# Normalised scores ahead of the queries' maximum, and gate sums in two float32r passes, in a fused attention and feed-forward kernel

## The chip, the cores and the metric

The kernel runs on one core of a Trainium2 chip. The metric is the device time of one execution in microseconds. A core has engines with queues of their own: PE (matrix products; its weight loads are listed apart as PEld), DVE, ACT and POOL (elementwise work), and SP, which here starts the DMAs. Each engine works through its queue in order and waits on semaphores for what other engines make.

## The reference

A block of a transformer on 2 sequences of 1024 tokens with 512 features, in float32:

```
x = x + layernorm(attention(layernorm(x)))
x = x + layernorm(ffn(layernorm(x)))

attention: q = x Wq (32 heads of 128), k = x Wk, v = x Wv (8 heads, each shared by 4 query heads)
  linear part:  qs = softmax(q), ks = softmax(k), gates gs = log_sigmoid(k) / 16
                per token: S = S * exp(gs) + ks v^T;  o_lin = qs S
  window part:  rope on q and k, softmax over the tokens of the own and the previous
                block of 64, masked to a distance of 64, times v
  o = 0.5 * window + 0.5 * o_lin, rounded to bfloat16, then times Wo
ffn: weights quantised to 16 levels in blocks of 64 and back;
     silu(x w1^T) * (x w2^T), then times w3^T
```

## The kernel before

**Work.** The attention part takes 8 key heads times 2 sequences times 8 stretches of 128 tokens, 128 *chunks* in all, in one loop over `n`. A chunk is one key head with its four query heads (`GRP`) on 128 tokens. Keys are made for two chunks at a time (`CB` = 2), so even and odd chunks differ: an even chunk makes the key products and key softmax of the pair to come (`key_products`, `key_softmax`), an odd chunk finishes them (`key_gates`, `key_decays`, `key_transposes`). Below, the numbering is from 0: `n` = 0 is even.

**Order.** Nothing plans the order. The attention's instructions are issued through `InOrder`, which keeps each engine's queue in program order, so the order of the calls in the loop is the order in each queue. All of these instructions are recorded on line 116, so the profile is read by tile names:

- `query_products(n + 1)`: PE makes `pq` (4 products of 512 columns); ACT copies it to `q`; POOL does the rope, `qtmp<-q,fcos`, two halves `qr<-q,fsin`, and `qr<-qr,qtmp`; DVE takes the negated maximum `nmq<-pq`.
- `query_exps`: four ACT exps of `pq` with `nmq` as bias. `query_softmax`: DVE `rsq`, then `qs<-pq,rsq`.
- `scores(n)`: PE `ps<-kT,qrT`. `score_masks`: DVE adds `fwin`, then the maximum `nms`. `score_exps`: four ACT exps of `ps`. `score_softmax`: DVE reciprocal `rss`, then the normalised scores `sw<-ps,rss`.
- `linear(n)`: PE `pa<-qh,kT`, `pa<-qh,khz`, `ot<-qh,S`. `mix`: PE transposes `sw` into `pa` (`pa<-ident,sw`); DVE masks `pa` to `A`. `values`: PE `ot<-A,vm`, `ot<-A,kv`. `heads`, `rounded_heads`: ACT `ob`, `oc`. `project`: PE `py<-wop,oc`, eight float32r products; `collect`: DVE `yacc`.
- `key_softmax`: ACT `kv`, then POOL rope `kr`, then POOL copies `vm`; DVE `nmk`; ACT `gate` = ln(1 + exp(-k)) and the exps `ke`. `key_gates`: PE `pg<-gate,fmid`, a float32 product of 256 columns with the constant `mid` (values of 0 and plus or minus 1/16), which sums the gates over tokens; ACT `ex` and `pg` exps. `key_decays`: DVE `kh`. `key_transposes`: PE `pt<-ident,kr`, `pt<-ident,kh`, `pg<-ident,ex`; ACT `kT`, `eq`, `em`.
- `query_transposes`: PE `tr<-ident,qr`, ACT copies it to `qrT`; PE `tq<-ident,qs`, which DVE turns into `qh` in the next chunk.
- `state_products`, `next_state`: PE `pS`, DVE `S`; the last chunk of a sequence has none.
- `signs` and `steps` spread the rounding of the feed-forward weights over the chunks: ACT signs `zs`, DVE steps on `zp` and `zm`. `part_weights` splits the output weights on POOL into float32r high and low parts (`wop`), in four chunks of each key head.

A float32 product stands in the trace as two instructions, a float32r one as one. PSUM pools have two buffers each (`pmm`: `pk`, `pq`, `pg`; `ptr`: `pt`, `tr`, `tq`; `psc`: `ps`, `pa`, `pS`; `po`: `ot`, `py`). After the attention comes the feed-forward part, with products of 512 columns.

Of the kernel before, what the change touches and what calls it, by code (L numbers as in the profile page):

```python
# [11 lines left out]
F32 = mybir.dt.float32  # L12
# [107 lines left out]
def sandwich_kernel(ctx: ExitStack, tc: tile.TileContext, x, wq, wk, wv, wo, w1, w2, w3, out, con):  # L120
# [141 lines left out]
    def fast_attention():  # L262

        with ExitStack() as attn:
# [62 lines left out]
            def load_const(name, shape, dtype, src):  # L327
                t = fc.tile(shape, dtype, name=name)
                nc.sync.dma_start(t, src)
                return t  # L330

            cosT = load_const("fcos", [P, NCH, D], F32, con["fcos"].rearrange("(c p) d -> p c d", p=P))
            sinT = load_const("fsin", [P, NCH, D], F32, con["fsin"].rearrange("(c p) d -> p c d", p=P))
            mid = load_const("fmid", [P, P], F32, con["fmid"])
            fwin = load_const("fwin", [P, 2, 4, P], BF16, con["fwin"])
            causal = load_const("fcausal", [P, 4 * P], F32, con["fcausal"])
            qb = load_const("fbounds", [P, 16], F32, con["bounds"])
# [17 lines left out]
            def row_max(src, n, tag):  # L355

                nm = fs.tile([P, n], F32, tag=f"nm{tag}", name=f"nm{tag}")
                vector.tensor_reduce(nm, src, AX.X, ALU.max, negate=True)
                return nm
# [29 lines left out]
            def key_softmax(n):  # L389

                c0, K = chunks[n][2], keys[n // CB]
                pk, before = K["pk"], K["before"]
                kv = kbuf.tile([P, CB, 2 * D], F32, tag="kv", name="kv")
                scalar.copy(kv, pk)
                k, v = kv[:, :, 0:D], kv[:, :, D : 2 * D]
                kr = ktmp.tile([P, CB, D], F32, tag="kr", name="kr")
                tmp = ktmp.tile([P, CB, D], F32, tag="tmp", name="tmp")
                rope(kr.unsqueeze(2), tmp.unsqueeze(2), k.unsqueeze(2), c0, CB, 1)

                vm = kbuf.tile([P, CB, D], F32, tag="vm", name="vm")  # L400
                gpsimd.tensor_copy(vm[0:W], v[0:W])
                gpsimd.tensor_copy(vm[W:P, 1:CB, :], v[W:P, 0 : CB - 1, :])
                if before is None:
                    gpsimd.memset(vm[W:P, 0, :], 0.0)
                else:
                    gpsimd.tensor_copy(vm[W:P, 0, :], before["v"][W:P, CB - 1, :])
                nm = row_max(pk[:, :, 0:D], CB, "k")

                gate = ktmp.tile([P, CB, D], F32, tag="gate", name="gate")
                scalar.activation(gate, pk[:, :, 0:D], AF.Exp, scale=-1.0)  # L410
                scalar.activation(gate, gate, AF.Ln, bias=1.0)
                ke = ktmp.tile([P, CB, D], F32, tag="ke", name="ke")
                sm = row_exps(ke, pk[:, :, 0:D], nm, CB, "k")
                K.update(v=v, vm=vm, kr=kr, gate=gate, ke=ke, sm=sm)

            def key_gates(n):

                K = keys[n // CB]
                pg = pmm.tile([P, 2, CB, P], F32, tag="mm", name="pg")
                product(pg[:, 0].rearrange("p j d -> p (j d)"), lhsT=mid, rhs=K["gate"].rearrange("p j d -> p (j d)"), start=True, stop=True)  # L420
                ex = ktmp.tile([P, CB, D], F32, tag="ex", name="ex")
                scalar.activation(ex, pg[:, 0], AF.Exp)
                ek = pg[:, 0]
                scalar.activation(ek, ek, AF.Exp, scale=-1.0)
                K.update(ex=ex, ek=ek, pe=pg[:, 1])
# [41 lines left out]
            def query_products(n):  # L467

                g, b, c = chunks[n]
                ci = b * NCH + c  # L470
                pq = pmm.tile([P, GRP, D], F32, tag="mm", name="pq")
                for kt in range(KT):
                    product(pq.rearrange("p h d -> p (h d)"), lhsT=xnT[:, kt, ci * P : (ci + 1) * P], rhs=weights[g][0][:, kt, :], start=kt == 0, stop=kt == KT - 1)
                q = q1p.tile([P, GRP, D], F32, tag="q", name="q")
                scalar.copy(q, pq)
                qr = q1p.tile([P, GRP, D], F32, tag="qr", name="qr")
                tmp = q1p.tile([P, GRP, D], F32, tag="qtmp", name="qtmp")
                rope(qr.unsqueeze(1), tmp.unsqueeze(1), q.unsqueeze(1), c, 1, GRP)
                Q[n] = {"pq": pq, "qr": qr, "nm": row_max(pq, GRP, "q")}

            def query_exps(n):

# [5 lines left out]
                vector.tensor_tensor(qs, Q[n]["pq"], rs.unsqueeze(2).to_broadcast([P, GRP, D]), ALU.mult)  # L488
                Q[n]["qs"] = qs

            def query_transposes(n):

                tr = ptr.tile([P, GRP, P], F32, tag="tr", name="tr")
                for h in range(GRP):
                    transpose(tr[:, h, :], Q[n]["qr"][:, h, :])
                qrT = q2p.tile([P, 2, GRP * W], F32, tag="qrT", name="qrT")
                scalar.copy(qrT.rearrange("p n (h t) -> p n h t", h=GRP), tr.rearrange("p h (n t) -> p n h t", n=2))
                tq = ptr.tile([P, GRP, P], F32, tag="tr", name="tq")
                for h in range(GRP):
                    transpose(tq[:, h, :], Q[n]["qs"][:, h, :])  # L500
                Q[n] = {"qrT": qrT, "tq": tq}

            def query_decays(n):
                j = n % CB
# [145 lines left out]
            key_softmax(0)  # L650
            key_sums(0)
            query_products(0)
            key_gates(0)
            key_decays(0)
            query_exps(0)
            query_softmax(0)
            key_transposes(0)
            query_transposes(0)

            BEGIN = (NCI - 2 * CB) // 2  # L660
            for n in range(N_):
                g, b, c = chunks[n]
                inputs = list(range(2 * CB + 2 * n, min(2 * CB + 2 * n + 2, NCI)))
                even = n % CB == 0
                more, keys2 = n + 1 < N_, n + CB < N_


                scores(n)
                if n:
                    rounded_heads(n - 1)  # L670
                score_masks(n)
                query_decays(n)
                if n:
                    next_state(n - 1)
                signs(2 if even else 1, n)
                steps(1, n)
                score_exps(n)
                if more:
                    query_products(n + 1)
                if even:  # L680
                    if more:
                        query_exps(n + 1)
                    signs(3, n)
                    score_softmax(n)
                    steps(1, n)
                    linear(n)
                    if keys2:
                        key_products(n + CB)
                    query_softmax(n + 1)
                    steps(1, n)  # L690
                    for ci in inputs[:1]:
                        input_norms(ci)
                    if keys2:
                        key_softmax(n + CB)
                    mix(n)
                    steps(1, n)
                    if keys2:
                        key_sums(n + CB)
                    if n:
                        project(n - 1)  # L700
                        collect(n - 1)
                    query_transposes(n + 1)
                    signs(1, n)
                    values(n)
                    heads(n)
                    steps(2, n)
                    for ci in inputs[1:]:
                        input_norms(ci)
                else:
                    if more:  # L710
                        key_gates(n + 1)
                        query_exps(n + 1)
                    signs(2, n)
                    score_softmax(n)
                    if more:
                        key_decays(n + 1)
                    linear(n)
                    mix(n)
                    if more:
                        query_softmax(n + 1)  # L720
                    project(n - 1)
                    collect(n - 1)
                    for ci in inputs[:1]:
                        input_norms(ci)
                    if more:
                        key_transposes(n + 1)
                    values(n)
                    if more:
                        query_transposes(n + 1)
                    heads(n)  # L730
                    steps(2, n)
                    for ci in inputs[1:]:
                        input_norms(ci)
                state_products(n)
                for ci in inputs:
                    input_transposes(ci)
                if b == 1 and c == 0 and g + 1 < KVH:
                    weights[g + 1] = load_weights(g + 1)
                if b == 1 and 2 <= c < 2 + GRP and g + 1 < KVH:
                    part_weights(g + 1, c - 2)  # L740
# [460 lines left out]
```

## Time and the profile before

| | |
|---|---|
| median of 3 runs | 2220.66 us (2218.14 to 2221.49) |
| the profiled execution | 2219.97 us |
| its span, first to last instruction | 2218.1 us |
| first scores (`ps`) of chunk 0, of chunk 127 | 55.5 us, 1701.1 us |
| even chunk, odd chunk, median from `ps` to `ps` | 13.84 us, 12.01 us |
| mean granted TensorE clock | 0.987 |

Some busy time on each engine stands in the page: PE 96%, DVE 67%, ACT 62%, POOL 42%. The lengths that the trace gives to matmuls overlap each other, so how long PE needs for a group is read from its start to the start of the next group. In a list of waits, `A <- B` means that engine and tile A sat idle until B ended, with the total, the number of times and the longest in us; in a timeline the idle time ahead of an instruction stands in brackets.

### The profile page before, as it was taken

The numbers are of one execution on the slowest core, as the hardware profiler recorded it, in microseconds if no ns is written. First come the engines' busy times: TensorE is split into PE (matmuls) and PEld (weight loads), VectorE is DVE, ScalarE is ACT, GpSimd is POOL, SyncE is SP. The second block draws the span as 40 slices with busy tenths as digits, with TensorE's granted clock in tenths as the row PEclk, the third lists the DMA queues.
The fourth block names the chain that finished last, engine by engine and source line by source line (L and its number), as shares of the span: only waits on it lengthen the run. The fifth ranks groups of instructions, "written<-read, shape, count | busy, mean of one in ns | idle before, by whom it ended". The sixth has DMA issues, their size and how long they took to land.

```text
span 2218.1 us, 27608 instructions
## 1 busy us (share of the span) xinstructions
PE 2132.0 (96%) x8948; PEld 1411.8 (64%) x8948; DVE 1484.3 (67%) x2822; ACT 1366.7 (62%) x3944; POOL 942.7 (42%) x1290
## 2 busy tenths in 40 slices
PE   4999999999999999999999999999998799999998
PEld 2667777777777767767777767776775454444443
DVE  3657788888778878778888878778886524232212
ACT  2568788787787888887778888788885210101000
POOL 3445555655465556446645655565553101000000
PEclk7999999999999999999999999999999899999999
DMA  5100100010010001000100010000000410000000
GB/s 200 34 15 10 58 11 15 25 48 10 9 41 26 15 15 58 10 10 10 58 14 15 21 49 11 12 10 17 10 12 19 143 44 34 5 29 1 19 0 21
DMA packets 45192, 64.52 MB, mean 29 GB/s; under 512 B 3632, under 2 KB 19632, under 8 KB 45040
## 3 DMA queue, kind: packets, MB, share of 16 engines
q1 hardware_dynamic: 45040, 62.67, 8.6%
q8 instruction: 73, 1.20, 0.2%
q14 instruction: 79, 0.65, 0.1%
HBM read 50.01 MB, written 12.65 MB: 28 GB/s over the span
## 4 chain that ended last, share of the span: by engine, by line
PE 67%; DVE 14%; ACT 14%; issue 2%; POOL 1%; DMA 1%; ACTq 0%; DVEq 0%; POOLq 0%; SPq 0%
PE py L116 9%; PE pq L116 8%; PE pk L116 7%; PE pgate L1125 7%; PE pf L1143 7%; PE pup L1125 7%; ACT ps L116 6%; PE ot L116 5%; PE ps L116 5%; PE pa L116 5%; DVE nmq L116 3%; DVE nms L116 2%; DVE ps L116 2%; DVE sw L116 2%; ACT q L116 2%; PE tr L116 2%
## 5 line engine op out<-in xcount | busy, mean ns | idle before, releaser
L116 PE MATMUL pq<-wq,xnT 128*128 128x512 f32 x1024 | 462.0, 594 | 0.0
L116 POOL TENSOR_TENSOR qtmp<-q,fcos 128x512 f32<-128x512 f32 x128 | 162.2, 1267 | 594.1 <-ACT q L116 594.1
L116 PEld LDWEIGHTS pq<-wq,xnT 128*128 128x128 f32 x1024 | 185.5, 191 | 184.5 <-issue 184.5
L116 ACT ACTIVATE zs<-xw,fbounds 128x512 bf16<-128x512 f32 (+3 forms) x416 | 288.2, 725 | 0.0
L116 PE MATMUL py<-wop,oc 128*128 128x512 f32 x1024 | 270.7, 406 | 1.3 <-ACT oc L116 1.3
L152 POOL TENSOR_TENSOR rstd<-ve,mhalf 128x1 f32<-128x1 f32 x64 | 35.8, 567 | 530.1 <-DVE ve L150 525.4
L116 ACT ACTIVATE ps<-ps,nms 128x128 f32<-128x128 f32 x512 | 175.0, 342 | 106.9 <-DVE nms L116 89.7
L116 PE MATMUL pk<-wkv,xnT 128*128 128x256 f32 x1024 | 233.8, 382 | 0.0
L1128 ACT ACTIVATE sg<-pgate 128x512 f32<-128x512 f32 (+1 forms) x44 | 26.3, 597 | 324.9 <-PE pgate L1125 324.9
L116 PEld LDWEIGHTS pk<-wkv,xnT 128*128 128x128 f32 x1024 | 196.2, 192 | 47.2 <-issue 14.1
L116 ACT ACTIVATE pq<-pq,nmq 128x128 f32<-128x128 f32 x512 | 175.1, 342 | 75.7 <-DVE nmq L116 63.2
L116 PEld LDWEIGHTS py<-wop,oc 128*128 128x128 f32 x1024 | 183.3, 189 | 36.5 <-ACT oc L116 1.7
L116 POOL TENSOR_TENSOR qr<-q,fsin 128x256 f32<-128x256 f32 x256 | 205.8, 825 | 0.0
L116 DVE SCALAR_TENSOR_TENSOR zp<-zp,zs 128x512 f32<-128x512 f32 (+3 forms) x224 | 195.4, 872 | 9.4 <-ACT zs L116 5.0
L116 POOL TENSOR_TENSOR qr<-qr,qtmp 128x512 f32<-128x512 f32 x128 | 166.4, 1300 | 9.8
L116 DVE TENSOR_TENSOR ps<-ps,fwin 128x512 f32<-128x512 f32 x128 | 89.3, 697 | 120.2 <-PE ps L116 119.5
L116 DVE SCALAR_TENSOR_TENSOR zm<-zm,zs 128x512 f32<-128x512 f32 (+3 forms) x192 | 163.3, 851 | 5.7 <-ACT zs L116 3.0
L116 DVE TENSOR_REDUCE nmq<-pq 128x4 f32<-128x512 f32 x128 | 88.5, 691 | 112.6 <-ACT q L116 112.6
L1125 PE MATMUL pgate<-x2T,w1T 128*128 128x512 f32 (+1 forms) x352 | 160.9, 595 | 0.0
L1125 PE MATMUL pup<-x2T,w2T 128*128 128x512 f32 (+1 forms) x352 | 158.2, 592 | 0.0
L1143 PE MATMUL pf<-w3T,hT 128*128 128x512 f32 (+1 forms) x352 | 151.8, 592 | 0.0
L116 PE MATMUL ps<-kT,qrT 128*128 128x128 f32 x1024 | 140.9, 281 | 9.9 <-ACT qrT L116 4.9
(125 smaller groups left out, 4077.2 us busy)
## 6 DMA issues: line engine op xcount, KB each, us to landing
wq<-in_L_attn_Wq_dram SPq DMA_DIRECT2D x8, 1024.0 KB, 6.3
wo<-in_L_attn_Wo_dram SPq DMA_DIRECT2D x8, 1024.0 KB, 5.1
xw<-in_L_ffn_w_dram SPq DMA_DIRECT2D x20, 256.0 KB, 2.6
dq<-zp SPq DMA_DIRECT2D x20, 256.0 KB, 2.0
row<-dq SPq DMA_DIRECT2D x20, 256.0 KB, 2.8
x<-_attn_hidden_states_dram SPq DMA_DIRECT2D x16, 256.0 KB, 2.8
xc<-_attn_hidden_states_dram SPq DMA_DIRECT2D x16, 256.0 KB, 2.7
out_dram<-res SPq DMA_DIRECT2D x16, 256.0 KB, 2.0
```

Of the source, the lines that this page charges most:

```text
L116: return lambda *args, **kwargs: self.tc.keep_in_program_order(getattr(self.engine, name)(*args, **kwargs))
L152: nc.gpsimd.tensor_tensor(rstd, ve, mhalf, ALU.pow)
L1125: nc.tensor.matmul(pg[:n, :], lhsT=wT[:, kt, f * P : f * P + n], rhs=x2T[:, kt, :], start=kt == 0, stop=kt == KT - 1)
L1128: nc.scalar.activation(sg[:n, :], ps[0][:n, :], AF.Sigmoid)
L1143: nc.tensor.matmul(pf, lhsT=hT[:n, f, m * P : (m + 1) * P], rhs=w3T[:n, f, :], start=f == 0, stop=f == NFT - 1)
```

## The change

Three things, in the attention part alone:

- In odd chunks `score_softmax(n)` (DVE `rss`, `sw`) comes ahead of the queries' maximum `nmq`, which has a function of its own, `query_max`; `key_decays` moves ahead of `signs(2, n)`. In even chunks the order stays.
- `query_transposes` is split in two. In odd chunks the rope part (`tr`, `qrT`) comes before `values`, and the softmax part (`tq`) stays behind it. `qrT` has one buffer instead of two.
- The gates are split on POOL into a float32r high part and the exact rest (`gates`, a copy and a subtraction, between `kr` and `vm`), and `pg` is the sum of two float32r products with `mid`, which is made float32r once by a DVE copy.

```diff
-            mid = load_const("fmid", [P, P], F32, con["fmid"])
+            mid = fc.tile([P, P], F32R, name="mid")
+            nc.vector.tensor_copy(mid, load_const("fmid", [P, P], F32, con["fmid"]))
...
                 rope(kr.unsqueeze(2), tmp.unsqueeze(2), k.unsqueeze(2), c0, CB, 1)
+                nm = row_max(pk[:, :, 0:D], CB, "k")
+
+
+                gate = ktmp.tile([P, CB, D], F32, tag="gate", name="gate")
+                scalar.activation(gate, pk[:, :, 0:D], AF.Exp, scale=-1.0)
+                scalar.activation(gate, gate, AF.Ln, bias=1.0)
+                gates = ktmp.tile([P, 2, CB, D], F32R, tag="gates", name="gates")
+                gpsimd.tensor_copy(gates[:, 0], gate)
+                gpsimd.tensor_tensor(gates[:, 1], gate, gates[:, 0].bitcast(F32), ALU.subtract)
...
-                nm = row_max(pk[:, :, 0:D], CB, "k")
-
-                gate = ktmp.tile([P, CB, D], F32, tag="gate", name="gate")
-                scalar.activation(gate, pk[:, :, 0:D], AF.Exp, scale=-1.0)
-                scalar.activation(gate, gate, AF.Ln, bias=1.0)
...
-                product(pg[:, 0].rearrange("p j d -> p (j d)"), lhsT=mid, rhs=K["gate"].rearrange("p j d -> p (j d)"), start=True, stop=True)
+                for i in range(2):
+                    product(pg[:, 0].rearrange("p j d -> p (j d)"), lhsT=mid, rhs=K["gates"][:, i].rearrange("p j d -> p (j d)"), start=i == 0, stop=i == 1)
...
-                Q[n] = {"pq": pq, "qr": qr, "nm": row_max(pq, GRP, "q")}
+                Q[n] = {"pq": pq, "qr": qr}
+
+            def query_max(n):
+                Q[n]["nm"] = row_max(Q[n]["pq"], GRP, "q")
...
-            def query_transposes(n):
+            def rope_transposes(n):
 
                 tr = ptr.tile([P, GRP, P], F32, tag="tr", name="tr")
                 for h in range(GRP):
                     transpose(tr[:, h, :], Q[n]["qr"][:, h, :])
-                qrT = q2p.tile([P, 2, GRP * W], F32, tag="qrT", name="qrT")
+                qrT = q2p.tile([P, 2, GRP * W], F32, tag="qrT", name="qrT", bufs=1)
                 scalar.copy(qrT.rearrange("p n (h t) -> p n h t", h=GRP), tr.rearrange("p h (n t) -> p n h t", n=2))
+                Q[n]["qrT"] = qrT
+
+            def softmax_transposes(n):
+
                 tq = ptr.tile([P, GRP, P], F32, tag="tr", name="tq")
...
                 else:
+                    score_softmax(n)
                     if more:
+                        query_max(n + 1)
                         key_gates(n + 1)
                         query_exps(n + 1)
+                        key_decays(n + 1)
                     signs(2, n)
-                    score_softmax(n)
-                    if more:
-                        key_decays(n + 1)
                     linear(n)
                     mix(n)
...
                     if more:
                         key_transposes(n + 1)
+                        rope_transposes(n + 1)
                     values(n)
                     if more:
-                        query_transposes(n + 1)
+                        softmax_transposes(n + 1)
                     heads(n)
```

More of the change, by code (lines that the diff above doesn't have):

```diff
@@ L406, in key_softmax @@
                     gpsimd.tensor_copy(vm[W:P, 0, :], before["v"][W:P, CB - 1, :])
-                nm = row_max(pk[:, :, 0:D], CB, "k")
-                gate = ktmp.tile([P, CB, D], F32, tag="gate", name="gate")
-                scalar.activation(gate, pk[:, :, 0:D], AF.Exp, scale=-1.0)
-                scalar.activation(gate, gate, AF.Ln, bias=1.0)
                 ke = ktmp.tile([P, CB, D], F32, tag="ke", name="ke")
                 sm = row_exps(ke, pk[:, :, 0:D], nm, CB, "k")
-                K.update(v=v, vm=vm, kr=kr, gate=gate, ke=ke, sm=sm)
+                K.update(v=v, vm=vm, kr=kr, gates=gates, ke=ke, sm=sm)
             def key_gates(n):
@@ L500, in query_transposes @@
                     transpose(tq[:, h, :], Q[n]["qs"][:, h, :])
-                Q[n] = {"qrT": qrT, "tq": tq}
+                Q[n] = {"qrT": Q[n]["qrT"], "tq": tq}
             def query_decays(n):
@@ L652, in fast_attention @@
             query_products(0)
+            query_max(0)
             key_gates(0)
@@ L657, in fast_attention @@
             key_transposes(0)
-            query_transposes(0)
+            rope_transposes(0)
+            softmax_transposes(0)
             BEGIN = (NCI - 2 * CB) // 2
@@ L680, in fast_attention @@
                 if even:
-                    if more:
-                        query_exps(n + 1)
+                    query_max(n + 1)
+                    query_exps(n + 1)
                     signs(3, n)
@@ L709, in fast_attention @@
                 else:
+                    score_softmax(n)
                     if more:
+                        query_max(n + 1)
                         key_gates(n + 1)
                         query_exps(n + 1)
+                        key_decays(n + 1)
                     signs(2, n)
-                    score_softmax(n)
-                    if more:
-                        key_decays(n + 1)
                     linear(n)
@@ L726, in fast_attention @@
                         key_transposes(n + 1)
+                        rope_transposes(n + 1)
                     values(n)
                     if more:
-                        query_transposes(n + 1)
+                        softmax_transposes(n + 1)
                     heads(n)
```

## The prediction

> **What bounds the kernel now.** I read the page first, then the waits over the attention part, then the timelines of PE, DVE, ACT and POOL over one pair of chunks, and last the starts of all 128 chunks in the PE timeline.
>
> ```profile
> PE 2132.0 (96%) x8948; PEld 1411.8 (64%) x8948; DVE 1484.3 (67%) x2822; ACT 1366.7 (62%) x3944; POOL 942.7 (42%) x1290
> ...
> PE 67%; DVE 14%; ACT 14%; issue 2%; POOL 1%; DMA 1%; ACTq 0%; DVEq 0%; POOLq 0%; SPq 0%
> ```
>
> PE looks full, but only 67% of the chain is PE: in some places DVE and ACT end last. The waits between 55 and 1702 us (total us, times, longest) name one for PE:
>
> ```profile
> PEld pa L116 <- DVE sw L116: 66.3, 64, 1.9
> ```
>
> 64 times, once a pair of chunks, the weight load of the score transposes (`pa<-ident,sw`) waits for the normalised scores `sw`. One odd chunk in the timelines (start us, length us) of PE, DVE, ACT and POOL:
>
> ```profile
> 543.35 1.06 PE L116 MATMUL ps<-kT,qrT 128*128 128x128 f32 x8
> ...
> 548.97 1.02 PE L116 MATMUL ot<-qh,S 128*128 128x512 f32 x2
> 550.11 0.66 PE L116 MATMUL pa<-ident,sw 128*128 128x128 f32 x4
> ...
> 553.98 0.60 PE L116 MATMUL tr<-ident,qr 128*128 128x128 f32 x4
> ...
> 554.86 0.39 PE L116 MATMUL pS<-kv,kh 128*128 128x128 f32 x2
> 555.35 0.79 PE L116 MATMUL ps<-kT,qrT 128*128 128x128 f32 x5
> ```
>
> ```profile
> 548.55 0.69 DVE L116 TENSOR_REDUCE nmq<-pq 128x4 f32<-128x512 f32 x1 [0.91 <-ACT q L116]
> 549.16 0.17 DVE L116 RECIPROCAL rss<-sms 128x4 f32<-128x4 f32 x1
> 549.36 0.69 DVE L116 TENSOR_TENSOR sw<-ps,rss 128x512 f32<-128x512 f32 x1
> ```
>
> ```profile
> 547.93 0.59 ACT L116 COPY q<-pq 128x512 f32<-128x512 f32 x1
> ```
>
> ```profile
> 548.66 1.27 POOL L116 TENSOR_TENSOR qtmp<-q,fcos 128x512 f32<-128x512 f32 x1 [4.13 <-ACT q L116]
> ...
> 551.39 1.31 POOL L116 TENSOR_TENSOR qr<-qr,qtmp 128x512 f32<-128x512 f32 x1
> ```
>
> Lengths of matmuls hold a latency, so I price PE from start to start. Two gaps are seen. `ot<-qh,S` needs 0.86 (the same group in even chunks) and the next starts after 1.14: `sw` ends at 550.05, because `rss` and `sw` stand behind `nmq`, which waited for ACT's copy of `q`, though the score exps had ended at 547.89. And `pS` needs 0.22, but the next scores come after 0.49, since ACT copies `qrT` out of `tr` only from 554.62 to 555.21. Even chunks (median 13.84) have neither gap; they only start slowly behind the late `qrT` (their `ps` takes 0.97 instead of 0.89). So 63 odd chunks, 767.8 us together, 12.01 typical, 12.19 mean, are what can shrink. The feed-forward part (after 1720 us) isn't touched.
>
> **The change part by part**, in us from the start of an odd chunk's `ps`.
>
> *`sw` before `nmq`.* Exps end at 4.55; `rss` and `sw` follow at the distances of the rows above (0.20 and 0.69): `sw` ends at 5.49, not 6.71. PE asks for it at 0.89 + 3.44 (`pq`) + 0.27 (`pg`, below) + 0.86 (`pa`) + 0.86 (`ot`) = 6.32: no wait. Behind it `nmq` ends at 6.10 instead of 5.89, so the four exps of `pq` and the two `zs` queued behind them on ACT end 0.21 later, at 9.3. `kT`, next on ACT, waits for `pt`, about 9.3 too: nothing lost. `qs` is then done at 9.0 and `tq` wanted at 10.7. On DVE `kh` moves from 7.74 to 6.9; `pt` wants it at 8.9.
>
> *The gates on PE.* Removed: two f32 instructions of 256 columns, 0.432. Added: two f32r ones. Not in the trace at that width; nearest is `py`, 8 f32r instructions of 512 columns from 550.52 to the next start at 552.46, 0.244 each. 256 columns stream in half the 0.215 that an f32 512-column instruction of one pass would take (0.43 for two), and `py` shows 0.03 on top: 0.137 each, 0.27. Bounds: 0.22 with nothing on top, 0.49 at `py`'s full price. I take 0.27, since `py` has the same type. By the Trainium skill's page "TensorE: Matmul & The Clock Gate" (§ Back-to-back issue gap, N/2.4 + 2.5 ns) it would be 0.22; `py`'s 244 ns against its 216 speaks for the overhead.
>
> *The rope transposes before `values`.* After `py` (1.95) and three pairs of key transposes (0.66), with 0.36 for `pa` unstalled as in even chunks, PE reaches `tr` at 6.32 + 0.36 + 1.95 + 0.66 = 9.29. Now it meets POOL: `qr` ends at 9.34 (median of the odd chunks; 9.27 least, 9.44 mean, 10.27 most), as ACT's `q` copy can't start before the score exps end. The trace shows this meeting once, in the last even chunk, which has no key products:
>
> ```profile
> 1697.51 1.28 POOL L116 TENSOR_TENSOR qr<-qr,qtmp 128x512 f32<-128x512 f32 x1
> 1698.84 0.66 PE L116 MATMUL tr<-ident,qr 128*128 128x128 f32 x4 [0.47 <-POOL qr L116]
> ```
>
> PE starts 0.05 after POOL's end, and `tr` then takes 0.49 to the next group instead of 0.44. So `tr` starts at the later of 9.28 and `qr` + 0.05; over the 63 chunks that is 9.49 on average, a new wait of 0.2. It is what is late next, and it makes most of the `pg` saving worthless: at 0.43 for `pg` the sum loses some 6 us, at 0.49 some 9. What waits in PE's queue behind `tr` is `values`, whose `A` has been ready since 7.7. `qrT` is then copied under `values`, so the wait before the next scores goes. Its single buffer costs nothing: the scores that read the old one end 9 us earlier.
>
> *Sum for odd chunks.* 63 x 9.49 + 48 x (0.49 + 0.86 + 0.44 + 0.22) + 15 x 1.79 (the last of a sequence has no `pS`) + 3 x 1.6 (input transposes) = 726.2, against 767.8: 41.6 saved. Even chunks start without the wait: 63 x 0.08 = 5.
>
> *POOL's two new instructions,* once a pair, between `kr` and `vm` in the even chunk. The subtraction is like `kr<-kr,tmp` (0.75), the copy between `kT<-kT` (0.25, 64 columns) and `vm` (0.77): together 1.0 to 1.5. POOL's next deadline is the odd chunk's `qtmp`; before it POOL idles 3.9 (median), 1.5 at least (where `wop` parts stand ahead), so the rope isn't pushed. `gates` is ready by 1 and `pg` wants it at 4.3. What can hurt is DVE: a `zp` step takes 0.69 alone, but 1.53 (median of 17) when it runs beside `qr<-qr,qtmp` alone, and 0.70 beside `vm` copies. Two `zp` steps stand at 542.60 to 544.13, ahead of the mask addition, which waits 0.31 for PE. After `kr` (542.78), a copy of some 0.4 and 0.75 more, the subtraction falls on the second step and can hold it to about 543.95, so the masks slip by some 0.06 typically; by 0 if the steps miss each other, by 0.75 - 0.31 = 0.44 if all of it blocks. In 25 of the 63 chunks the masks already start after 1.15 instead of 1.09, and no cushion is left: there I take 0.2, between nothing and the 0.44 and nearer to the typical slip, as some of these wait for a `zs` of ACT anyway. 38 x 0.06 + 25 x 0.2 = 7. A slip goes through exps, `q` and rope straight into `tr`.
>
> *Startup.* One DVE copy of `mid` (a 128x128 `S` copy is 0.28) and 1.2 more ahead of the first rope on POOL, which ends at 52.74 with the first scores at 55.47, where `qs` (54.45) was last: 0 to 1.2, I take 0.6. No DMA moves.
>
> Total: 41.6 + 5 - 7 - 0.6 = 39. The profiled run took 2219.97 (span 2218.1 and 1.9 around it), 0.7 below the median of the runs, within their spread: **2181**.
>
> **Rivals.** *B, the rope ends as late in odd chunks as in even ones.* In even chunks `qr` ends at 9.82, as DVE's two-input steps run beside it. If `yacc` and steps, moved earlier, or late masks put the odd chunk there too, `tr` starts 0.4 to 0.45 later: 63 x 0.43 = 27 less gain, 2208, or 2201 if the masks' slip is a part of it. Against it: between 5.3 and 9.3 DVE has in odd chunks only work that reads PSUM, and keeps it. 0.19.
>
> *C, slower: `gates` holds up the masks.* If both new POOL instructions shut DVE out for their full length, both `zp` steps wait, and the masks slip by 1.0 to 1.5 less the 0.31. It decides from 46 / 63 = 0.73 a chunk; at 1.1 the loss is 63 x 0.37 = 23: 2243. For it: 1.53 beside a two-input POOL instruction. Against: 0.70 beside copies, and `kr` is nearly always over when the first step runs. By the Trainium skill, "SBUF — State Buffer" (§ SBUF: two separate sides), a DVE instruction with two SBUF inputs and any POOL instruction that reads SBUF exclude each other for the whole instruction; that rule speaks for C, and the rows beside `vm` don't bear it out. 0.07.
>
> *D, nothing gained:* the wait for `sw` only moves to `tr`. With `qr` at 10.06 the odd chunk is as long as now; 4 of 63 have that or come within 0.12 of it. 2216 to 2224. 0.04.
>
> *E, better:* neither DVE nor POOL slips, and masks late today come on time because odd-chunk work ends earlier: 2219.97 - 46 (the sum without its debits) - 6 (63 x 0.1, the mean of `qr`'s end down to its median) = 2168. 0.10.
>
> **How the numbers follow.** Forecast 0.60 (2172 to 2190), B 0.19, E 0.10, D 0.04, C 0.07. Leaving out C, D and the edge of E leaves some 0.83 between 2166 and 2208, which also takes in both ends of `pg`. B's own chance lies at its upper end. About 0.2% (4.4 us) can be told from no change: faster 0.89, same 0.04, slower 0.07.
>
> **What would show it.** PE's wait for `sw` gone from the list, a new one `tr <- POOL qr` of about 0.1 to 0.2 in most odd chunks, none for `qrT`; odd chunks at 11.4 to 11.7, even ones at 13.76; `pg` 0.27 to the next start. The mask addition later than 1.15 in odd chunks would show B or C; a `gates` subtraction over 1 us or `zp` steps over 1 us at the end of even chunks would show the port. It is wrong if odd chunks stay near 12, or if a new PE wait in even chunks appears.

## The result

| | median of the runs | profiled execution |
|---|---|---|
| before | 2219.4 us (2216.4 to 2221.49, 4 runs) | 2219.97 us, span 2218.1 |
| after | 2182.56 us (2181.02 to 2183.9, 4 runs) | 2182.67 us, span 2180.9 |

The ratio is 0.9835, with a 95% interval of 0.9818 to 0.9852: faster by 37 us, with the same granted clock (0.986 after, 0.987 before). The 64 even chunks together took 874.0 us (877.8 before) and the 63 odd ones 733.7 (767.8); the first scores started at 56.27 (55.47). That is -3.8 - 34.1 + 0.8 = -37.1, and the span lost 37.2: nothing else moved.

### The profile after

The page of the kernel after, engines and the chain that ended last:

```profile
PE 2107.5 (97%) x8948; PEld 1401.8 (64%) x8948; DVE 1500.0 (69%) x2823; ACT 1358.5 (62%) x3944; POOL 1021.8 (47%) x1418
...
PE 76%; ACT 7%; DVE 7%; POOL 6%; issue 1%; DMA 1%; ACTq 0%; POOLq 0%; DVEq 0%; SPq 0%
```

DVE and ACT have 7% of the chain each where they had 14%, and POOL went from 1% to 6%. The first says that the old wait is gone, the second that a new one came: POOL does nothing in the chain but the rope. The waits of PE and of its weight loads between 56 and 1665 us (total us, times, longest):

```profile
PEld tr L116 <- POOL qr L116: 22.4, 58, 0.9
PEld pa L116 <- DVE sw L116: 19.8, 44, 1.4
...
PE tr L116 <- POOL qr L116: 8.3, 22, 0.5
...
PE pa L116 <- DVE sw L116: 1.2, 4, 0.5
```

Among the waits for another engine `tr <- POOL qr` is now the longest, where it was `sw` before. A wait of PEld is not yet one of PE, since loads run ahead of the products: `sw` still makes a load wait 44 times, but PE itself 4 times. The same odd chunk as in the prediction, PE first:

```profile
533.42 1.06 PE L116 MATMUL ps<-kT,qrT 128*128 128x128 f32 x8
...
537.34 0.80 PE L116 MATMUL pg<-gates,mid 128*128 128x256 f32 x2
537.99 0.59 PE L116 MATMUL pa<-qh,kT 128*128 128x256 f32 x2
...
538.85 1.02 PE L116 MATMUL ot<-qh,S 128*128 128x512 f32 x2
539.71 0.60 PE L116 MATMUL pa<-ident,sw 128*128 128x128 f32 x4
...
542.81 0.66 PE L116 MATMUL tr<-ident,qr 128*128 128x128 f32 x4
543.30 0.60 PE L116 MATMUL ot<-A,vm 128*128 128x256 f32 x2
...
544.61 0.39 PE L116 MATMUL pS<-kv,kh 128*128 128x128 f32 x2
544.83 0.39 PE L116 MATMUL ps<-kT,qrT 128*128 128x128 f32 x2
```

Then DVE and POOL:

```profile
538.20 0.69 DVE L116 TENSOR_TENSOR sw<-ps,rss 128x512 f32<-128x512 f32 x1
538.81 0.68 DVE L116 TENSOR_REDUCE nmq<-pq 128x4 f32<-128x512 f32 x1
```

```profile
538.73 1.26 POOL L116 TENSOR_TENSOR qtmp<-q,fcos 128x512 f32<-128x512 f32 x1 [3.03 <-ACT q L116]
541.47 1.29 POOL L116 TENSOR_TENSOR qr<-qr,qtmp 128x512 f32<-128x512 f32 x1
```

Both old gaps are closed: `ot<-qh,S` needs 0.86 to the transposes of `sw` (538.85 to 539.71), and `pS` 0.22 to the next scores (544.61 to 544.83). `tr` starts at 542.81, 0.05 after `qr` ended (541.47 + 1.29): this is the meeting with POOL. The chunk takes 11.41, where it took 12.00.

### The profile page after: what moved, and what is told of

Its sections match the earlier page's. It is cut to its first block, busy times and chain, and to the rows that moved or that the text cites. A ratio compares the mean times of both kernels' runs of the same rounds, so it can differ in the third digit from the quotient of the medians.

```text
span 2180.9 us, 27690 instructions
## 1 busy us (share of the span) xinstructions
PE 2107.5 (97%) x8948; PEld 1401.8 (64%) x8948; DVE 1500.0 (69%) x2823; ACT 1358.5 (62%) x3944; POOL 1021.8 (47%) x1418
## 4 chain that ended last, share of the span: by engine, by line
PE 76%; ACT 7%; DVE 7%; POOL 6%; issue 1%; DMA 1%; ACTq 0%; POOLq 0%; DVEq 0%; SPq 0%
PE pq L116 15%; PE pk L116 8%; PE ot L116 7%; PE pgate L1142 7%; PE py L116 7%; PE pf L1160 7%; PE pup L1142 7%; PE pa L116 5%; PE ps L116 5%; POOL qr L116 4%; PE tr L116 3%; ACT ps L116 3%; PE tq L116 2%; POOL qtmp L116 2%; ACT q L116 1%
## 5 line engine op out<-in xcount | busy, mean ns | idle before, releaser
L116 DVE SCALAR_TENSOR_TENSOR zm<-zm,zs 128x512 f32<-128x512 f32 (+3 forms) x192 | 169.6, 883 | 5.4 <-ACT zs L116 3.0
```

Source lines behind the costliest of these rows:

```text
L116: return lambda *args, **kwargs: self.tc.keep_in_program_order(getattr(self.engine, name)(*args, **kwargs))
```

## The experiments

Times are medians; ratios are to the kernel before on the same chip, with 95% intervals. "Masks" is the mean start of the mask addition in the odd chunks and "`tr`" that of the rope transposes, both from the start of the chunk's `ps`; the changed kernel has 1.35 and 9.57, the kernel before 1.25 and 10.74.

**e1, the order without the gates.** The changed kernel, with `pg` again one float32 product of the unsplit `gate`.

```diff
-                gpsimd.tensor_copy(gates[:, 0], gate)
-                gpsimd.tensor_tensor(gates[:, 1], gate, gates[:, 0].bitcast(F32), ALU.subtract)
-                for i in range(2):
-                    product(pg..., lhsT=mid, rhs=K["gates"][:, i]..., start=i == 0, stop=i == 1)
+                product(pg..., lhsT=mid, rhs=K["gate"]..., start=True, stop=True)
```

> The changed kernel with the gates as before: one float32 product, no split on POOL. Theory (the wait for sw and the wait for qrT were the gain, POOL's rope now sets tr, the float32r passes are hidden behind that wait): pg takes 0.43 again, PE is ready for tr at 9.45 instead of 9.29, still about where the rope ends (9.39); the masks start 0.10 earlier on average, as POOL has two instructions less. 2175 to 2182, as fast as the changed kernel or some us faster. Rival (PE is the bound all through, so every PE saving counts): 63 x 0.19 = 12 us slower than the changed kernel, 2195.

Measured: 2176.42 us, 0.9808 (0.9795 to 0.9822). Odd chunks together 728.4, masks 1.25, `tr` 9.54. The order alone gains 43 us, more than the whole change.

**e2, the gates without the order.** The kernel before with the split on POOL and the two float32r passes; `qrT` has one buffer, to make room for `gates`.

```diff
+                gpsimd.tensor_copy(gates[:, 0], gate)
+                gpsimd.tensor_tensor(gates[:, 1], gate, gates[:, 0].bitcast(F32), ALU.subtract)
```

> The kernel before with the gate split and the float32r passes alone, order as before (one qrT buffer, to make room). Theory: PE saves 0.19 ahead of a wait for sw that ends when DVE ends, so nothing of it is left; the odd masks slip by 0.1 on average and sw with them: 2219 to 2227, no gain. Rival (PE savings count): 2207.

Measured: 2224.34 us, 1.0026 (1.0015 to 1.0036): slower by 5 us. In the waits of this kernel the load of the score transposes has

```profile
PEld pa L116 <- DVE sw L116: 83.5, 64, 2.1
```

against 66.3 before: PE comes earlier by 12 us (63 x 0.19) and waits 17 more, since the masks start at 1.35 instead of 1.25 and push `sw` back. Odd chunks together grew from 767.8 to 773.1. The passes are shorter, and nothing is waiting for them.

**e3 and e4, one half of the order each,** on the kernel before. In e3 `score_softmax(n)` stands first in the odd chunk; in e4 the rope transposes stand before `values`.

```diff
 e3
+                    score_softmax(n)
                     if more:
                         query_max(n + 1)
 ...
-                    score_softmax(n)
 e4
                         key_transposes(n + 1)
+                        rope_transposes(n + 1)
                     values(n)
                     if more:
-                        rope_transposes(n + 1)
                         softmax_transposes(n + 1)
```

> The kernel before with score_softmax ahead of the queries' maximum in odd chunks alone: rope transposes behind values, gates as before. Theory: the wait for sw goes, tr starts at 10.31 instead of 10.64 (10.74 on average), the wait for qrT at the end of the odd chunk stays (0.49 after pS): odd chunks 11.68, 26 us less in all, 2193. Rival (the wait only moves on to the next late thing): 2215 to 2220.

> The kernel before with the rope transposes ahead of values in odd chunks alone: sw behind nmq, gates as before. Theory: PE comes to tr at 9.78 as the wait for sw stays, after the rope's end (9.34), so no new wait; the wait for qrT goes: odd chunks 11.74 typical, even ones 13.76, 24 us less, 2196. Together with sw first it gives less than the sum of both (26 + 24 = 50 against some 41), because then the rope is late. Rival (the moved transposes wait for the rope in any order): 2210 or more.

Measured: e3 2193.51 us, 0.9884 (0.9869 to 0.9899); e4 2196.13 us, 0.9900 (0.9885 to 0.9915). With 2219.81 for the kernel before in these runs, the halves gain 26.3 and 23.7, 50 in sum, and together 43.4 (e1). Where do the other 7 go? In the odd chunks the weight load of `tr` waited for `qr` twice in e3, four times in e4 and 19 times in e1. From start to start these waits come to 5.3 us in e1, and `tr` itself, which takes 0.49 behind such a wait instead of 0.44, to 1.3 more. Only with both halves does PE often reach `tr` before POOL is done. (As in the changed kernel, both runs have one `qrT` buffer, and e3 has `key_decays` ahead of `signs(2, n)`.)

**e5, the rope made shorter.** The changed kernel without the last POOL addition of the queries' rope.

```diff
-                gpsimd.tensor_tensor(dst, dst, tmp, ALU.add)
+                if heads == 1:
+                    gpsimd.tensor_tensor(dst, dst, tmp, ALU.add)
```

> The changed kernel without the last addition of the queries' rope on POOL (qr keeps the sine part alone, so the window scores are of other numbers). Theory (tr waits for POOL's rope and for nothing else): qr ends about 1.3 earlier, at 8.1, PE's wait for it goes, tr starts at 9.29 in every odd chunk, odd chunks 11.25 with pS, mean 11.3: 63 x 0.33 = 21 us less than the changed kernel, 2160 to 2164. Rival (tr is held by PE's own queue, and the wait in the list is only named after POOL): within 5 us of the changed kernel.

Measured: 2159.53 us, 0.9728 (0.9713 to 0.9743), 23 us less than the changed kernel. No wait for `qr` is left, `tr` starts at 9.28, where the prediction had PE ready (9.29), and odd chunks together take 715.2, 18.5 less; even ones give 1.9 and the first rope some 3, which I had left out; so the time is a little below my 2160, though the odd chunks gained less than the 21 that I expected. The wait for POOL cost 18 us: in most odd chunks the end of `qr` set when `tr` could start.

**e8, the gates behind the copies of `vm`.** The changed kernel with the two new POOL instructions moved three instructions later, out of the way of the `zp` and `zm` steps.

```diff
-                gpsimd.tensor_copy(gates[:, 0], gate)
-                gpsimd.tensor_tensor(gates[:, 1], gate, gates[:, 0].bitcast(F32), ALU.subtract)
                 vm = kbuf.tile([P, CB, D], F32, tag="vm", name="vm")
 ...
+                gpsimd.tensor_copy(gates[:, 0], gate)
+                gpsimd.tensor_tensor(gates[:, 1], gate, gates[:, 0].bitcast(F32), ALU.subtract)
```

> The changed kernel with POOL's two gate instructions behind the vm copies instead of ahead of them. Theory (the subtraction holds up the last zp steps of DVE ahead of the masks, and copies don't): the steps run beside vm again, as before the change, the odd masks are back at 1.25 on average from 1.35, the rope 0.07 earlier: 4 to 6 us less than the changed kernel, 2177 to 2179. Rival (any POOL work there holds DVE up alike): same as the changed kernel, 2182.

Measured: 2175.57 us, 0.9799 (0.9786 to 0.9812): 7 us less than the changed kernel, where I had expected 4 to 6, and level with e1. Masks 1.27, `tr` 9.46, odd chunks together 727.0. The tile `gates` in the changed kernel and, in the second fence, in e8 (ns: least/median/most):

```profile
L116 POOL CAST gates<-gate x63: 388/860/981, 70.1 to 1639.8; 128x256 fp32r<-128x256 f32 x63
L116 POOL TENSOR_TENSOR gates<-gate,gates x63: 722/1053/1292, 70.6 to 1640.7; 128x256 fp32r<-128x256 f32 x63
```

```profile
L116 POOL CAST gates<-gate x63: 397/397/930, 69.4 to 1633.5; 128x256 fp32r<-128x256 f32 x63
L116 POOL TENSOR_TENSOR gates<-gate,gates x63: 722/726/1056, 70.2 to 1634.3; 128x256 fp32r<-128x256 f32 x63
```

In the old place the pair took 1.9 us beside DVE's steps, in the new one 1.1 (medians). What it did to DVE is seen in one odd chunk, the changed kernel first (PE's scores, DVE, POOL):

```profile
432.88 1.06 PE L116 MATMUL ps<-kT,qrT 128*128 128x128 f32 x8
```

```profile
433.46 1.26 DVE L116 SCALAR_TENSOR_TENSOR zp<-zp,zs 128x512 f32<-128x512 f32 x1 [0.35 <-ACT zs L116]
434.64 0.69 DVE L116 TENSOR_TENSOR ps<-ps,fwin 128x512 f32<-128x512 f32 x1
```

```profile
433.44 0.73 POOL L116 TENSOR_TENSOR gates<-gate,gates 128x256 fp32r<-128x256 f32 x1
```

and the same chunk in e8:

```profile
430.59 1.06 PE L116 MATMUL ps<-kT,qrT 128*128 128x128 f32 x8
```

```profile
431.17 0.79 DVE L116 SCALAR_TENSOR_TENSOR zp<-zp,zs 128x512 f32<-128x512 f32 x1 [0.35 <-ACT zs L116]
431.88 0.69 DVE L116 TENSOR_TENSOR ps<-ps,fwin 128x512 f32<-128x512 f32 x1
```

```profile
430.17 1.95 POOL L116 COPY vm<-kv 64x256 f32<-64x256 f32 x3
```

Here ACT's `zs` comes last, so the step starts late in both kernels, 0.58 after the scores. In the changed kernel it starts 0.02 after the subtraction, takes 1.26 and ends 0.55 behind the subtraction's end (434.72 against 434.17), and the masks start at 1.76 (434.64 - 432.88). In e8 the `vm` copy that is running when it starts (the third, merged with the others in its row) ends at 431.41; the step takes 0.79, ends 0.55 behind that, and the masks start at 1.29. So the step waits for the POOL instruction that is under way in both kernels, and a copy is only shorter. My theory for e8, that copies don't hold DVE up, is not what the trace shows (more in the last section).

Chunk by chunk against e1, the masks of the changed kernel are later by 0.07 to 0.70 in 20 of the 63 odd chunks and within 0.03 in all others but one (0.15 earlier): 6.6 us together. The two kernels stand 6.2 apart, 5.4 of it in the odd chunks. In 18 of the 20 the subtraction is under way when one of the last steps ahead of the masks starts, in six of them since `zs` came late.

**e6 and e7, `values` split.** The first product of `values` (`ot<-A,vm`) goes ahead of the rope transposes and the second stays behind, so that POOL has 0.43 more. e6 is the changed kernel with this, e7 is e1 with this.

```diff
+                    values(n, (0,))
+                    if more:
                         rope_transposes(n + 1)
-                    values(n)
+                    values(n, (1,))
```

> The changed kernel with the first product of values (ot with vm, 0.43) ahead of the rope transposes in odd chunks and the second behind them. Theory: PE reaches tr at 9.72 instead of 9.29, after the rope's end in 45 of 63 chunks; tr starts at 9.78 on average, and 1.55 after it the next scores start, with qrT copied by then (tr + 1.23): odd chunks 11.34 on average instead of 11.65: 19 us less than the changed kernel, 2163. Rival (the qrT copy ends too late for the next scores once tr is later): the gap comes back there, 2175 or more.

> The same split of values, with the gates as one float32 product and no split on POOL. Theory: PE reaches tr at 9.91, hardly ever before the rope; now nothing hides the 0.19 of pg, so this is 0.11 a chunk better than the order alone with float32 gates (2176), 2169, and 6 us slower than the split of values with float32r gates. Rival (float32r gates cost 6 us in any order, as POOL's two instructions do the harm): 6 us faster than with float32r gates, 2157.

Measured: e6 2169.39 us, 0.9772 (0.9757 to 0.9787); e7 2172.12 us, 0.9784 (0.9769 to 0.9799). `tr` starts at 9.78 in e6, as expected, but the odd chunk takes 11.43 in the mean instead of 11.34, so my figure of 2163 was missed by 6. The waits show a part of it, one for `tq`, whose PSUM buffer is freed by ACT's copy `kT`; in the changed kernel it was 1.3 us, 6 times:

```profile
PEld tr L116 <- POOL qr L116: 8.8, 23, 0.9
...
PEld tq L116 <- ACT kT L116: 2.7, 7, 0.6
```

Read from start to start, all of the 6 us stand behind the start of `tr`, in four pieces of 1 to 2 us: `tr` itself, the start of `tq`, the scores after `pS`, and the scores after `tq` in the chunks that have no `pS`. Why the last two are late stays open. e7 was to be 2169 and 6 slower than e6; it is 2.7 slower. Small as that is, every run of e6 is faster than every run of e7: once PE has other work to do while POOL finishes, the float32r passes shorten the kernel, though the masks still slip.

**e9, e10 and e11, the repairs together.** e9 is e6 with the gates behind `vm` as in e8. On the same chip and in the same runs stood e10, the changed kernel itself, and e11, e1 again.

> The changed kernel with both: the first product of values ahead of the rope transposes, and POOL's gate instructions behind the vm copies. Theory: tr starts at the later of 9.72 and the rope's end + 0.05, 9.75 on average with the masks at 1.27; ACT's kT and qrT come late in fewer chunks than in the split of values alone; odd chunks 11.37 on average, 4 us less than the split of values alone and even chunks 1.5 less: 2164, and 8 us faster than the same split with float32 gates (2172), so that the float32r passes then pay most of their 12 us. Rival (the two repairs don't add up, since PE is full in both): 2169.

> The changed kernel itself, on the same chip as the version with both repairs: 2182, odd chunks 11.65, to set the differences of a few us against.

> The changed kernel with float32 gates, on the same chip as the changed kernel. Theory: 5 to 7 us faster than the changed kernel, as in the traces (728.4 us in odd chunks against 733.8). Rival (the difference between the two was one of chips): same within 3 us.

| | median | ratio |
|---|---|---|
| e9, both repairs | 2166.64 us (2165.8 to 2167.37) | 0.9758 (0.9745 to 0.9772) |
| e10, the changed kernel | 2182.88 us (2180.18 to 2182.97) | 0.9830 (0.9816 to 0.9843) |
| e11, order without gates | 2175.37 us (2172.47 to 2177.46) | 0.9794 (0.9781 to 0.9807) |

e10 against e11 repeats the finding of e1: in the order of the change its split gates cost 7.5 us. e9 beats both kernels, by 53 us the one before and by 16 the changed one, and it is 5.5 below e7, which ran on another chip. I had expected 2164 and 8 us: with the repairs the float32r passes pay about half of the 12 us that they take off PE, not most. What the split does to the time thus went from +5 (e2) over +7 (e10 against e11) and about 0 (e8 against e1, 0.9 apart, within their spreads) and -2.7 (e6 against e7) to -5.5 (e9 against e7), with the same instructions each time.

## Why the prediction was right, and where its steps were off

**Right in mechanism.** The two gaps closed (the one ahead of `sw`'s transposes in all but 6 odd chunks, the one ahead of the next scores in all but 7), `tr` became the place where PE meets POOL, odd chunks shrank, even ones gained only at their `ps`, and the result is within 2 us of the forecast. Rivals B and D needed `qr` as late as 9.8 or 10.06; its mean end went from 9.44 to 9.52. C needed a slip of the masks above 0.73; the mean was 0.10. E needed none; e8 comes near to that (1.27 against 1.25), but at 2175.57 it is still 7.6 us above E's 2168. One of the signs misled: masks later than 1.15 were to show B or C, and their median came to 1.22 without either.

**`sw` ends at 5.49.** It did at the least (5.48); the median is 5.79, still ahead of the 6.32 at which PE asks. In 6 chunks `sw` ends later than that, and `ot<-qh,S` needs 0.88 in the mean instead of 0.86: 1.4 us in all that the sum didn't have.

**`tr` at the later of 9.28 and `qr` + 0.05, 9.49 on average, a new wait of 0.2.** With the masks' slip of 0.11 this makes 9.60; measured 9.57, and a wait of 0.28 (from the last key transposes to `tr` 0.50 in the mean instead of 0.22). e5 confirmed the one end: without the wait `tr` starts at 9.28. The sum of 726.2 and 7 for the slip makes 733; 733.7 was measured.

**`pg` at 0.27.** The last `pq` and `pg` together took 0.861 to the start of `pa` before and 0.669 after, 0.19 less, so two float32r passes of 256 columns cost 0.43 - 0.19 = 0.24, between my value and the estimate of 0.22 from the Trainium skill's page "TensorE: Matmul & The Clock Gate" (§ Back-to-back issue gap); the trace cannot tell the 0.03 between them from the blur of the pipeline.

**"At 0.43 for `pg` the sum loses some 6 us": a wrong sum.** With the ends of `qr` in the kernel before, the later of 9.44 and `qr` + 0.05 is 0.046 above the 9.49 of the forecast, which makes 2.9 us over 63 chunks; at 0.49 for `pg` it makes 5.6 and not 9. The runs lost less still. e1 has `pg` at 0.43, and against e8, which has the passes and the masks almost on time, its odd chunks took 728.4 to 727.0: 1.4 us. Its `tr` starts 5.0 us later, summed over the chunks, but 3.7 of them come back behind that start: in 43 of the 63 chunks PE finds POOL done, and `tr` then takes 0.44 instead of the 0.49 that my sum has in every chunk (2.2 us).

**The masks' slip of 38 x 0.06 + 25 x 0.2 = 7: right in sum by luck, wrong in its parts.** The runs show 6.6, but in 20 chunks of 0.34 on average, and nearly nothing in the others. Typical chunks lose nothing: there the steps run ahead of the subtraction, and the pair of `zp` steps takes 1.53 with and without it. Chunks pay where one of the last steps ahead of the masks starts while it is under way; in 12 of the 20 the masks of e1 were not late at all (1.09 to 1.14), so that lateness, by which I had told the 25 chunks from the 38, was not the mark. The longest slip, 0.70, is beyond my bound of 0.44, which had the cushion of the typical chunk in it.

**POOL's two instructions, 1.0 to 1.5: mis-sized.** They took 1.9 (0.86 and 1.05, medians), because most of them wait for a DVE step that is under way; in e8, where few do, the medians are 0.40 and 0.73. The cover was large enough: POOL's idle time before the odd chunk's `qtmp` fell from 3.9 to 3.0 (median), and 0.35 was left where it is least.

**Even chunks, 63 x 0.08 = 5:** 3.8 measured, because the scores of 9 even chunks still take 0.97; before the change 60 did. **Startup, 0.6:** 0.8 measured, but the first scores of one and the same kernel moved by 1.3 between two profiles (55.85 in e1, 57.12 in e11), so this term is not shown by the runs.

**The rule behind C, and why C did not come.** The Trainium skill's page "SBUF — State Buffer" (§ SBUF: two separate sides) has a DVE instruction of two SBUF inputs and a POOL instruction that reads SBUF exclude each other: the one that starts first keeps the port for its whole length, and the other waits. I had read the rows beside `vm` as speaking against that. They agree with it: 0.35 left of a `vm` copy made a step of 0.90, and 0.70 left of the subtraction one of 1.25. Two things of C's price were wrong instead. A step that has started is not held, and in typical chunks the steps start first; and what a step waits for is what is left of one POOL instruction, not the length of both.

## What to carry to other kernels

Time taken off the bounding engine is worth nothing in front of a wait, and what pays for it on another engine can then make the kernel slower: price both sides, in the order in which they stand. When two waits are closed together, the next one is whatever was second at the later place, here the rope on POOL; look for its cover (half of `values`) and for what feeds it (the masks) in the same step. And a slip of a chain is to be priced chunk by chunk, not from the typical one: ask which of two instructions that exclude each other is under way when the other starts, and how much of it is left.

## What was not expected of the hardware

A DVE step with two inputs in SBUF and a POOL instruction that reads SBUF take turns, whatever the POOL instruction does. The `zp` and `zm` steps of 512 columns on 128 partitions show it; there are 260 of them in the changed kernel. Of these, 116 started with less than 0.14 us left of any such POOL instruction and took 0.68 to 0.69. The other 144 started with more left, and all but three took what was left plus 0.55, within 0.01: for the subtraction 0.70 and 1.25, for the cast 0.34 and 0.88, for a `vm` copy 0.35 and 0.90. (In the three, the two started within 0.04 us of each other, the step took 0.68 or 0.69, and POOL waited.) One copy and one step, from the changed kernel:

```profile
292.50 0.53 POOL L116 COPY khz<-kT 128x128 f32<-128x128 f32 x1 [0.44 <-ACT kT L116]
292.80 0.78 DVE L116 SCALAR_TENSOR_TENSOR zp<-zp,zs 128x512 f32<-128x512 f32 x1
```

The step ends 0.55 after the copy (293.58 against 293.03). The added time is that of the wait and not of the step's size: in three of the 20 slipping chunks a step of a few columns (`zra`) took 0.69 or 0.70 instead of 0.26, because it had to wait for the subtraction. In the other direction POOL waits too: its cast went from 0.40 to 0.86 and its subtraction from 0.73 to 1.05 behind DVE steps under way. The mask addition, of whose two inputs one lies in PSUM, holds nothing up: in e8 all 45 casts that started during it took 0.40. That is why the place behind `vm` is the better one: there the last steps meet pieces of 0.29 and 0.39, and the gates run beside the masks. The order of POOL's queue alone, with the same instructions, decided 7 us of this kernel.
